# Layer 3's weight products as seven block products, new durations in the planner, and a changed merge of the left products: a four-layer graph network on one core

## The chip, the cores and the metric

The kernel runs on one core of a Trainium2 chip. Five engines work side by side: TensorE (PE, matrix products, with its own weight-load row PEld), VectorE (DVE), ScalarE (ACT), GpSimd (POOL) and SyncE (SP), whose queue here only issues DMA transfers. Each takes its instructions in a fixed order and waits on semaphores for the others. The metric is the device time of one execution, in microseconds (us); lower is better.

## The reference, cut to what matters

Sixty-four graphs of 256 nodes with 128 features (`x`, float32) pass through four layers that share one 0/1 adjacency matrix `adj` of 256 x 256. Each layer adds its result to its input and applies a layer norm. Layers 0 and 1 are attention layers, layer 2 is a gated network of five steps, layer 3 a sum of adjacency powers with weights:

```python
x = _layernorm(x + _L0_gnn_ref(x, adj, ...))      # attention over pairs
x = _layernorm(x + _L1_gnn_ref(x, adj, ...))      # attention, elu
x = _layernorm(x + _L2_gnn_ref(x, adj, adj, ...)) # five gated steps
# layer 2, one step
m_in = jnp.einsum('nm,bmd->bnd', in_matrix, h)    # adj @ h; m_out is the same
z = sigmoid(av @ w3_w.T + u3);  r = sigmoid(av @ w4_w.T + u3)
hv = tanh(av @ w5_w.T + (r * h) @ u5_w.T);  h = (1 - z) * h + z * hv
# layer 3: parts x, adj x, adj^2 x, adj^3 x, again adj x ... (adj1 is adj)
x_all = jnp.concatenate([x, chebyshev(adj, x, 3), chebyshev(adj, x, 3)], axis=3)
y = jnp.einsum('bnik,iok->bno', x_all, weight_1)  # layer norm of x + y is the output
```

With the two copies of each power put together, and the residual `x` folded into the first weight, layer 3 is y = x W0 + (A x) W1 + A^2 (x W2 + (A x) W3). The kernel forms a = A x first, then both bracketed sums with the weights, and then one product with A^2.

## The kernel before, in words

**Units and lanes.** The 64 graphs are handled in 32 units of two graphs (`UB = 2`); a unit's data is a tile of 128 partitions x 512 columns: two graphs x 256 nodes x 128 features, cut into blocks of 128 x 128. Ten lanes (`LANES`) hold the buffers of ten units in flight; unit u uses lane u mod 10. All of PSUM is eight banks of 512 columns, given to tiles by the planner.

**The planner.** The program first only lists tasks: `add(engine, ns, function, reads, writes, ...)`. `Plan.run` then lays all tasks out as a list scheduler does: for each engine it takes, among the tasks whose inputs are ready by its own clock and for which banks are free, the one with the lowest key (`first`, from the unit's number, the task's due time and `HASTE`). Its clock uses the `ns` given with each task and fixed latencies between engines. Only the order that results is written into the program: the durations in `add` are no work on the chip, but they decide where every instruction stands. `TAIL` sets how the last ten units are staggered. `PLAIN` is the number of last units that use a plain form of layer 3 (`layer3_end`).

**Seven products for eight.** A product of two matrices cut into 2 x 2 blocks takes eight block products; Winograd's form takes seven, with sums of blocks before and after. The kernel uses it for the products with A (`left_fast`, lines 838 to 861) in layer 2 and layer 3: three block sums of the data on GpSimd (`block_sums`, lines 833 to 836), seven matmuls of 128 columns (line 844), then four adds on VectorE (`merged`, lines 872 to 878), with the first product copied out of PSUM by ScalarE (line 856). The block sums of the matrix itself are made once (`fast_blocks`). The product with A^2 in layer 3 uses the same form (line 1015).

**Layer 2** (line 882 on) runs five steps per unit: A h by `left_fast`, five products of 512 columns with gate weights (line 902), three activations, four VectorE updates, and a turn of the state between node-major and feature-major by a VectorE 32 x 32 transpose and a DMA to DRAM and back. `turned` (line 537) does the same before layers 2 and 3: a transpose (line 546), one write to DRAM (line 549) and four gathers (line 552).

**Layer 3** (line 985 on), for all but the last three units: eight products of 256 columns with the two weights side by side (line 1004), into two banks; ScalarE copies the part that A^2 will multiply out of PSUM (lines 1009, 1010); VectorE makes its block sums; seven products with the blocks of A^2 (line 1015) follow, and `merged` and one more add (line 1035) put the results together. Then layer norm (`layernorm`, line 581) and the store. `layer3_end` does eight weight products (line 1048) and four of 256 columns with A^2 (line 1055).

The softmax here doesn't subtract the row's maximum and nothing guards it: scores larger than these inputs give would overflow.

## Time and profile before

| What | Value |
|---|---|
| Time, median of 3 runs | 1391.08 us (1391.00 to 1391.69) |
| The profiled execution's own time | 1392.14 us |
| Its span, first to last instruction | 1390.3 us |
| TensorE clock granted | 1.000 |
| TensorE busy | 1379.5 us (99%) |
| VectorE busy | 1217.7 us (88%) |
| ScalarE busy | 909.1 us (65%) |
| GpSimd busy | 630.5 us (45%) |
| DMA | 147 MB moved, mean 106 GB/s |

"Busy" is the time in which at least one instruction of the engine is under way. Matmuls overlap each other, so the length of a record is longer than the distance between two. A row of the groups reads: line, engine, operation, output <- inputs, shapes, count | busy us, mean ns of one | idle time of the engine just before it and what ended it. The waits list who waited for whom: us in total, times, longest. The chain that ended last follows the run back from its last instruction.

### The profile page before, as it was taken

How to read it: one execution, taken by the hardware profiler on the slowest of the kernel's cores; microseconds unless marked ns; L12 is line 12 of the kernel's file. 1: busy time of each engine (PE TensorE's matmuls, PEld its weight loads, DVE VectorE, ACT ScalarE, POOL GpSimd, SP SyncE). 2: the span in 40 equal slices, each digit the busy share in tenths (PEclk: the TensorE clock that was granted, in tenths of full speed). 3: DMA queues.
4: the chain of work that ended last, by engine and by line, in shares of the span. 5: the costliest groups of instructions: out<-in, count | busy, mean ns of one | idle time of the engine just before them, and what ended most of it. 6: DMA issues, size and time to landing. Idle time of an engine off the chain costs nothing.

```text
span 1390.3 us, 23222 instructions
## 1 busy us (share of the span) xinstructions
PE 1379.5 (99%) x6891; PEld 967.8 (70%) x6891; DVE 1217.7 (88%) x2745; ACT 909.1 (65%) x2121; POOL 630.5 (45%) x1039
## 2 busy tenths in 40 slices
PE   9999999999999999999999999999999999999998
PEld 8776666677667777667767767776666666666777
DVE  6887999999888989989898999899889798988955
ACT  6988554655676676865776768877675556564544
POOL 4233344345354453544453554465444443644524
PEclk9999999999999999999999999999999999999999
DMA  4223454445454545554554544455544545544422
GB/s 119 49 60 95 98 113 98 116 109 121 107 121 106 118 105 114 122 118 112 112 117 105 124 111 113 105 111 125 118 106 98 114 108 104 123 100 107 104 64 61
DMA packets 530076, 147.12 MB, mean 106 GB/s; under 512 B 456480, under 2 KB 495136, under 8 KB 529952
## 3 DMA queue, kind: packets, MB, share of 16 engines
q1 hardware_dynamic: 529152, 145.13, 46.5%
q8 instruction: 55, 0.90, 0.3%
q14 instruction: 69, 0.57, 0.1%
q10 hardware_dynamic: 800, 0.52, 0.1%
HBM read 81.10 MB, written 64.46 MB: 105 GB/s over the span
## 4 chain that ended last, share of the span: by engine, by line
PE 94%; DVE 3%; ACT 1%; POOL 0%; issue 0%; DMA 0%; POOLq 0%; SPq 0%; DVEq 0%; ACTq 0%
PE ps L902 48%; PE ps L844 20%; PE ps L1004 7%; PE ps L780 4%; PE ps L743 4%; PE ps L1015 3%; PE ps L792 2%; PE ps L738 2%; PE ps L667 2%; PE ps L821 1%; PE ps L1048 1%; PE ps L1055 0%; DVE st L587 0%; PE ps L351 0%; PE ps L968 0%
## 5 line engine op out<-in xcount | busy, mean ns | idle before, releaser
L902 PE MATMUL ps<-m,gT 128*128 128x512 f32 x960 | 471.5, 593 | 0.9 <-DVE m L878 0.5
L902 PEld LDWEIGHTS ps<-m,gT 128*128 128x128 f32 x960 | 170.3, 190 | 136.8 <-issue 115.9
L589 POOL TENSOR_SCALAR ve<-st 128x4 f32<-128x4 f32 x110 | 34.9, 317 | 364.9 <-DVE st L587 347.1
L914 ACT ACTIVATE e<-ps,bias 128x512 f32<-128x512 f32 x160 | 109.7, 686 | 130.2 <-PE ps L902 125.8
L931 ACT ACTIVATE p<-ps,bias 128x512 f32<-128x512 f32 x160 | 110.0, 687 | 90.3 <-PE ps L902 87.7
L592 POOL TENSOR_TENSOR rstd<-ve,nhalf 128x4 f32<-128x4 f32 x126 | 145.6, 1156 | 43.8 <-DVE ve L589 33.7
L902 PE MATMUL ps<-e,u5T 128*128 128x512 f32 x320 | 163.4, 593 | 0.0
L922 ACT ACTIVATE e<-ps,bias 128x512 f32<-128x512 f32 x160 | 109.7, 686 | 80.7 <-PE ps L902 78.6
L844 PE MATMUL ps<-adjTp,e 128*128 128x128 f32 x968 | 148.2, 275 | 0.4 <-ACT e L856 0.4
L933 DVE SCALAR_TENSOR_TENSOR p<-e,p 128x512 f32<-128x512 f32 x160 | 117.2, 733 | 33.1 <-ACT p L931 32.1
L844 PEld LDWEIGHTS ps<-adjTp,e 128*128 128x128 f32 x968 | 131.0, 192 | 19.0 <-issue 14.5
L833 POOL TENSOR_TENSOR e<-ht 128x256 f32<-128x256 f32 x121 | 99.4, 821 | 89.0 <-DMA ht<-hb 67.9
L844 PEld LDWEIGHTS ps<-adjTp,ht 128*128 128x128 f32 x726 | 108.7, 191 | 40.8 <-issue 36.7
L844 PE MATMUL ps<-adjTp,ht 128*128 128x128 f32 x726 | 120.8, 275 | 0.0
L902 PEld LDWEIGHTS ps<-e,u5T 128*128 128x128 f32 x320 | 59.2, 190 | 65.9 <-issue 50.1
L611 ACT ACTIVATE x<-ht,ve,rstd 128x128 f32<-128x128 f32 x212 | 90.9, 487 | 13.9 <-POOL ve L600 13.6
L902 PE MATMUL ps<-xT,gT 128*128 128x512 f32 x192 | 98.3, 593 | 0.5 <-DVE m L872 0.5
L833 POOL TENSOR_TENSOR e<-x 128x256 f32<-128x256 f32 x61 | 48.2, 790 | 96.2 <-ACT x L611 83.9
L875 DVE TENSOR_TENSOR m<-ps,m 128x256 f32<-128x256 f32 x182 | 74.8, 413 | 13.4 <-PE ps L844 11.1
L769 ACT ACTIVATE e<-m,esd 128x256 f32<-128x256 f32 x116 | 84.5, 765 | 0.0
L872 DVE TENSOR_TENSOR m<-ps,e 128x256 f32<-128x256 f32 x182 | 74.4, 413 | 11.2 <-PE ps L844 6.9
L835 POOL TENSOR_TENSOR e<-e,ht 128x128 f32<-128x128 f32 x121 | 79.4, 657 | 5.9
(210 smaller groups left out, 3145.7 us busy)
## 6 DMA issues: line engine op xcount, KB each, us to landing
hb<-p SPq DMA_DIRECT2D x182, 256.0 KB, 2.1
ht<-hb SPq DMA_DIRECT2D x484, 64.0 KB, 2.5
xT<-hb SPq DMA_DIRECT2D x244, 64.0 KB, 2.5
m<-row SPq DMA_DIRECT2D x58, 256.0 KB, 3.6
hb<-p SPq DMA_DIRECT2D x124, 64.0 KB, 1.8
ht<-hb SPq DMA_DIRECT2D x31, 256.0 KB, 3.0
out_dram<-x SPq DMA_DIRECT2D x30, 256.0 KB, 2.4
m<-in_x_dram SPq DMA_DIRECT2D x88, 64.0 KB, 2.3
```

The costliest lines, as they stand in the source:

```text
L592: add(POOL, 1050, lambda: nc.gpsimd.tensor_tensor(rstd.ap, ve.ap, nhalf.ap, op=ALU.pow), (ve, nhalf), (rstd,))
L611: add(ACT, 400, lambda j=j, b=b, ch=ch, view=view, at=at, shift=shift, col=col: nc.scalar.activation(X[u].ap[:, b, ch, :], view()[:, j, :] ...
L769: add(ACT, 600, lambda g=g, b=b: nc.scalar.activation(e.ap[:, g, :].rearrange("p (c n) -> p c n", c=NC), ev()[:, b], AF.Prelu, bias=esd.ap ...
L833: add(by, wide, lambda: eng.tensor_sub(four[:, 0:2], blk(slice(2, 3)).to_broadcast([P, 2, D]), blk(slice(0, 4, 3))), (src,), (s,), group=ss)
L835: add(by, narrow, lambda: eng.tensor_sub(four[:, 2:3], four[:, 1:2], blk(slice(0, 1))), (src, s), (s,), group=ss)
L844: add(PE, mm_ns(P) + 4, lambda: nc.tensor.matmul(ps.ap[:, at * P : (at + 1) * P], lhs(), mat.ap[:, k, c * P : (c + 1) * P], start=True, st ...
L902: add(PE, mm_ns(T), lambda: nc.tensor.matmul(ps.ap, w(), rhs.ap, start=start, stop=stop, skip_group_check=True), (c, rhs), (ps,), after)
L914: add(ACT, 600, lambda ps_g=ps_g, up=up: nc.scalar.activation(r.ap, ps_g.ap, AF.Tanh, bias=bias2.ap[:, 1:2], scale=0.5 / up), (ps_g, bias2 ...
L922: add(ACT, 600, lambda ps_g=ps_g, up=up: nc.scalar.activation(z.ap, ps_g.ap, AF.Tanh, bias=bias2.ap[:, 0:1], scale=0.5 / up), (ps_g, bias2 ...
L931: add(ACT, 600, lambda ps_v=ps_v, up=up: nc.scalar.activation(v.ap, ps_v.ap, AF.Tanh, bias=bias2.ap[:, 2:3], scale=1 / up), (ps_v, bias2), ...
L933: add(DVE, 600, lambda: nc.vector.scalar_tensor_tensor(v.ap, z.ap, 1.0, v.ap, op0=ALU.add, op1=ALU.mult), (v, z), (v,))
L1004: add(PE, mm_ns(N), lambda k=k, src=src, c=c, b=b, ps=ps, at=at: nc.tensor.matmul(gd(ps.ap)[:, at], bn(src.ap)[:, b, c * P : (c + 1) * P], ...
```

## The change

Five things change together.

1. Layer 3's weight products are done by seven block products too, each of 128 columns and done for the two halves of the rows (`layer3_blocks`, fourteen matmuls). The two rows of blocks are the two graphs, the inner blocks are x and A x, the two columns of blocks the two weight sums. GpSimd makes four sums of x and A x before, and VectorE four adds after them; the block sums that the A^2 product needs are now made by GpSimd. Products that are only added to each other add up in PSUM: later matmuls write without `start` onto columns that an earlier one filled, after ScalarE has copied what is needed alone. It takes four banks instead of two. The output takes five VectorE adds.
2. `left_fast` lets its second product add onto the first in PSUM, after ScalarE has copied the first out; ScalarE then copies the sum, and VectorE's first merge handles one block instead of two.
3. `turned` transposes with its input read in order and writes to DRAM by four transfers of 128-byte runs, then reads back by one plain transfer (before: one plain write, four gathers).
4. The planned durations are set anew for nearly all tasks; `TAIL` goes from 0.3 to 0.2 and `HASTE` from 10e3 to 15e3.
5. `PLAIN` goes from 3 to 4, and in `layer3_end` the two halves of a bank change places, as do the weights in `w3`.

```diff
-TAIL = 0.3
+TAIL = 0.2
...
-HASTE = {"pe": 10e3, "act": 10e3, "dve": 10e3}
-PLAIN = 3
+HASTE = {"pe": 15e3, "act": 15e3, "dve": 15e3}
+PLAIN = 4
...
+        for name, at in (("U", 0), ("p1", 2 * P)):
+            c[name] = Cell(c["z"].ap[:, at : at + 2 * P], over=[c["e"], c["z"]])
...
+    fast_blocks(w3f, w3)
...
-        add(DVE, 1050, lambda: nc.vector.transpose(
+        add(DVE, 625, lambda: nc.vector.transpose(
             v.ap.rearrange("p (a g i) -> p g a i", g=G, i=BL),
-            X[u].ap.rearrange("p b c (j a) -> p (b c) a j", j=BL)), (X[u],), (v,))
-        add("sp", 560, lambda: nc.sync.dma_start(L["hb"].ap, v.ap), (v,), (L["hb"],))
+            X[u].ap.rearrange("p b c (a j) -> p (b c) a j", j=BL)), (X[u],), (v,))
         parts = object()
         for q in range(P // BL):
-            add("sp", 640, lambda q=q: nc.sync.dma_start(
-                t.ap.rearrange("p (g q i) -> p g q i", g=G, i=BL)[:, :, q],
-                L["hb"].ap[q * BL : (q + 1) * BL].rearrange("j (a g i) -> (j a) g i", g=G, i=BL)),
-                (L["hb"],), (t,), group=parts)
+            add("sp", 560, lambda q=q: nc.sync.dma_start(
+                L["hb"].ap.rearrange("(j a) (g q i) -> q j (a g) i", a=D // BL, g=G, i=BL)[q],
+                v.ap[q * BL : (q + 1) * BL].rearrange("j (a g i) -> j (a g) i", g=G, i=BL)), (v,), (L["hb"],), group=parts)
+        add("sp", 450, lambda: nc.sync.dma_start(t.ap, L["hb"].ap.rearrange("(j a) n -> a j n", a=D // BL)), (L["hb"],), (t,))
...
-        one(x, 0, a(0), 0, 0, (src,))
-        add(ACT, 280, lambda: nc.scalar.copy(p1.ap[:, 0:P], x.ap[:, 0:P]), (x,), (p1,))
-        one(x, 1, a(1), 1, 0, (src,))
-        one(y, 3, a(3), 3, 1, (src,), s.writers[-1:])
+        one(x, 0, a(0), 0, 0, (src,), start=True)
+        held = [add(ACT, 160, lambda: nc.scalar.copy(p1.ap[:, 0:P], x.ap[:, 0:P]), (x,), (p1,))]
+        one(x, 0, a(1), 1, 0, (src,), held)
+        ms = object()
+        add(ACT, 160, lambda: nc.scalar.copy(gd(m.ap)[:, 0], x.ap[:, 0:P]), (x,), (m,), group=ms)
+        one(y, 3, a(3), 3, 1, (src,), s.writers[-1:], start=True)
...
-        merged(x, y, p1, m)
-
-    def merged(x, y, p1, m):
+        add(DVE, 200, lambda: nc.vector.tensor_add(gd(m.ap)[:, 3], gd(x.ap)[:, 2], p1.ap[:, 0:P]), (x, p1), (m,), group=ms)
+        merged(y, m, ms)
+
+    def merged(y, m, ms):
...
-        add(DVE, 400, lambda: nc.vector.tensor_tensor(
-            mv[:, 0:4:3], pv(x)[:, 1:3], p1.ap[:, 0:P].rearrange("p (o n) -> p o n", o=1).to_broadcast([P, 2, P]), op=ALU.add),
-            (x, p1), (m,))
...
-        x, y = bank(), bank()
-        home = {(0, 0): (x, slice(0, 2)), (1, 1): (x, slice(2, 4)), (0, 1): (y, slice(0, 3, 2)), (1, 0): (y, slice(1, 4, 2))}
...
+        layer3_blocks(u, L, xT, aT, tail)
+
+    def layer3_blocks(u, L, xT, aT, tail):
+        x, ya, yb, z = bank(), bank(), bank(), bank()
...
+        for k, (cell_, i, op, j, cells) in enumerate((
+                (sa, x1, ALU.subtract, x0, (xT,)), (sa, x1, ALU.subtract, a1, (xT, aT)),
+                (sb_, sums[1], ALU.subtract, x0, (sa, xT)), (sb_, sums[2], ALU.add, a0, (sb_, aT)))):
+            add(POOL, 780, lambda k=k, i=i, op=op, j=j: nc.gpsimd.tensor_tensor(sums[k], i, j, op=op), cells, (cell_,), group=group)
...
+        late = sb_.writers[-2:-1]
+        for c in range(NC):
+            one(x, 2 * c, blk(x0, c), (xT,), w3f, 0, start=not c, after=tail)
+        held = [add(ACT, 270, lambda: nc.scalar.copy(gd2(p1.ap), gd2(x.ap)[:, 0:3:2]), (x,), (p1,))]
+        for c in range(NC):
+            one(x, 2 * c, blk(a0, c), (aT,), w3f, 2, after=held)
+        for c in range(NC):
+            one(x, 2 * c + 1, blk(sums[2], c), (sb_,), w3f, 5)
+        for c in range(NC):
+            one(ya, c, blk(sums[1], c), (sa,), w3f, 4, start=not c, after=late)
...
+        for c in range(NC):
+            one(yb, NC + c, blk(a1, c), (aT,), w3f, 7)
+        m4 = gd2(mv.ap)
+        add(DVE, 335, lambda: nc.vector.tensor_add(gd2(up.ap), gd2(x.ap)[:, 1:4:2], gd2(p1.ap)), (x, p1), (up,))
+        add(DVE, 600, lambda: nc.vector.tensor_add(
+            mv.ap.rearrange("p (k n) -> p k n", k=2), ya.ap.rearrange("p (k n) -> p k n", k=2),
+            up.ap.rearrange("p (o n) -> p o n", o=1).to_broadcast([P, 2, N])), (ya, up), (mv,))
+        add(DVE, 335, lambda: nc.vector.tensor_add(up.ap, ya.ap[:, 0:N], mv.ap[:, N : 2 * N]), (ya, mv), (up,))
+        add(DVE, 600, lambda: nc.vector.tensor_add(mv.ap, yb.ap, mv.ap), (yb, mv), (mv,))
...
+        add(POOL, 780, lambda: nc.gpsimd.tensor_sub(f[:, 0:2], E[:, 4:5].to_broadcast([P, 2, P]), E[:, 0:6:5]), (mv, up), (four,), group=fs)
+        add(POOL, 580, lambda: nc.gpsimd.tensor_sub(f[:, 2:3], f[:, 1:2], E[:, 0:1]), (mv, four), (four,), group=fs)
+        add(POOL, 580, lambda: nc.gpsimd.tensor_add(f[:, 3:4], f[:, 2:3], E[:, 1:2]), (mv, four), (four,), group=fs)
...
+        one(z, 0, None, (mv,), a2f, 0, e_(0), True)
+        add(ACT, 160, lambda: nc.scalar.copy(p1.ap[:, 0:P], z.ap[:, 0:P]), (z,), (p1,))
+        done = [one(x, 0, None, (mv,), a2f, 2, e_(1)), one(x, 2, None, (four,), a2f, 3, f_(3))]
+        done = [one(x, 3, None, (up,), a2f, 7, e_(5), True, done)]
...
+        add(DVE, 335, lambda: nc.vector.tensor_add(o[:, 1:3], gd2(x.ap)[:, 2:4], o[:, 1:3]), (x, out), (out,))
+        add(DVE, 335, lambda: nc.vector.tensor_add(o[:, 2:4], o[:, 2:4], m4[:, 2:4]), (out, mv), (out,))
```

## Prediction

> **What bounds the kernel now.** I read the page first (share of each engine), then TensorE's waits, then the chain of work that ended last, then the rows of the single groups. The page's first part:
>
> ```profile
> PE 1379.5 (99%) x6891; PEld 967.8 (70%) x6891; DVE 1217.7 (88%) x2745; ACT 909.1 (65%) x2121; POOL 630.5 (45%) x1039
> ...
> PE 94%; DVE 3%; ACT 1%; POOL 0%; issue 0%; DMA 0%; POOLq 0%; SPq 0%; DVEq 0%; ACTq 0%
> PE ps L902 48%; PE ps L844 20%; PE ps L1004 7%; PE ps L780 4%; PE ps L743 4%; PE ps L1015 3%; PE ps L792 2%; PE ps L738 2%; PE ps L667 2%; PE ps L821 1%; PE ps L1048 1%; PE ps L1055 0%; DVE st L587 0%; PE ps L351 0%; PE ps L968 0%
> ```
>
> TensorE is 94% of the chain, and L1004, the line that the change replaces, 7% of it. The waits of TensorE, whole:
>
> ```profile
> PE ps L351 <- POOL ident masks.py:199: 1.3, 1, 1.3
> PE ps L792 <- DVE m L872: 0.7, 1, 0.7
> PE ps L667 <- ACT xT L535: 0.6, 1, 0.6
> PE ps L902 <- DVE m L878: 0.5, 1, 0.5
> PE ps L576 <- DVE cu L674: 0.5, 1, 0.5
> PE ps L902 <- DVE m L872: 0.5, 1, 0.5
> PE ps L844 <- ACT e L856: 0.4, 1, 0.4
> PE ps L902 <- ACT e L914: 0.2, 1, 0.2
> PE ps L792 <- ACT xT L783: 0.2, 1, 0.2
> ```
>
> Nine waits, 4.9 us (1.3 + 0.7 + 0.6 + 3 x 0.5 + 0.4 + 2 x 0.2) in 1390. About half of it lies in the first 40 us; the rest is six waits, five of them between 171 and 301 us. So almost every microsecond is a matmul being issued, and the price of a product is its spacing. The chain in order of time gives it (start, length, what):
>
> ```profile
> 143.24 3.57 PE ps L844 x32
> ...
> 278.41 3.45 PE ps L1004 x16
> ...
> 1383.19 1.15 PE ps L1055 x4
> ...
> 1384.42 0.44 DVE st L629
> ```
>
> An fp32 product is two records. A 128-column product costs 3.57/16 = 0.223 us, a 256-column product of L1004 3.45/8 = 0.431 us. The last two rows: TensorE ends at 1384.3, and about 6 us of layernorm and store follow in any case.
>
> **What the Trainium skill says.** "Trainium Kernel Development and Optimization", Performance Expectations: matmul busy time is a bad metric, because matmuls are pipelined. The trace agrees: 1379.5 us are "busy", but the products counted times their spacing (800 of 512 columns x 0.858, 450 of 256 x 0.431, 2122 of about 128 x 0.2224, 123 transposes x 0.11) are 1368, so I cost by spacing. "PSUM — Partial Sum Buffer", The four PSUM rules: a write without the first-matmul flag adds where the element was written since the last such flag, and overwrites elsewhere. So the new products can add into columns that an earlier one filled, at no extra instruction; L1015 before does the same at the plain 0.22 us. "SBUF — State Buffer", Who interferes with whom: a VectorE instruction with two SBUF inputs and a GpSimd instruction that reads SBUF exclude each other. The trace agrees: the update at L933 averages 733 ns and took 0.67 us at the quiet end of the run. "DMA: Bandwidth & Descriptors", Specifications: under 512 B a transfer is done by read-modify-write; used below as an upper bound.
>
> **The change, part by part.**
>
> *TensorE, weight products of layer 3.* Units 0 to 27 each drop eight 256-column products (3.453 us) and get fourteen of 128 columns (14 x 0.2224 = 3.114): -0.339 x 28 = -9.49 us. Unit 28 moves to the plain end form (PLAIN 3 to 4): same eight weight products, but four 256-column a2 products instead of seven blocks: 4 x 0.4315 - 7 x 0.2224 = +0.17. The seven products of `left_fast` and of a2 stay seven. Sum -9.32 us.
>
> *The second product of `left_fast` now adds onto the first one* and must let ScalarE copy the first result out. It is the only new kind of wait on TensorE in the main loop, 182 times, and all later matmuls queue behind it. The copy started 0.42 us after the issue of its product ended (1363.25 to 1363.67), lasts 0.27 (L856), and from the end of a copy to the next matmul it took 0.06 plus 0.11 of weight load (1383.13 to 1383.30): 0.86 us. Counted in the built order of the new kernel, TensorE has at least 0.88, at 5% of the places 1.08 and at the median 1.7 us of other products in between. So it fits, narrowly in some 30 places. Before, L902 behind the tanh of L914 has 31 such narrow places and one wait of 0.2 us. I take 0.3 us; from 0 to 30 x 0.15 = 4.5.
>
> *VectorE.* `left_fast`: one 256-column add (413 ns) becomes a 128-column one (279): -0.134 x 182 = -24 us. Transpose at L546: 1113 ns with strided reading; L943 reads in order and takes 701: -0.41 x 61 = -25. Layer 3: dropped 439 + 351 + 340 + 415 + 411 + 278 + 403 + 276 = 2.91 us x 29; new, by the rows of like operations, 5 x 0.413 + 2 x 0.69 + 0.28 + 0.44 = 4.17 us x 28: +32. Net -17 us before port contention.
>
> *GpSimd* gets five small operations once, for the block sums of the weights (about 2.7 us by the rows of L481 and L484, needed only at the first L1004 product, 179 us into the run), and per unit five operations of 256 columns (about 0.81) and two of 128 (0.64): 5.3 us x 28 = +149, 630 to 780 us, 56%. Its elementwise work grows from 371 to 520 us. If VectorE's loss to the shared port, 55 ns per two-input operation now, grows with it, that is +22 ns on some 830 operations: +18 us. VectorE stays where it is, near 1218 us, 88%. *ScalarE*: 182 copies more (0.27) = +48, layer 3 1.00 to 0.63 us: net +37, 68%. None of these three is on the chain; if they were, their waits would show as TensorE's.
>
> *`turned`*: one write and four gathers of 128-byte runs become four writes of 128-byte runs and one plain read. Five SP issues as before, but now one read waits for all four landings. No row shows such a write. Nearest: four writes of 512-byte runs (L961), 1.8 us; upper bound, twice the 2.5 us of the old gathers, 5 us. Path: 0.7 + 4 x 0.5 of issue + 1.8 to 5 + 3.0 (256 KB read) = 7.5 to 10.7 us; one of two writes per unit is on the way of a product. In the new order at least 11.5 us of products stand between the transpose and the first product on its result (before 12.6), 15 at a quarter of the places. Cost: zero.
>
> *PSUM*: layer 3 holds four banks instead of two, and its first one from the weight products to the end; the planner takes that into account by the order, so it costs only where the order leaves TensorE short. *New planned durations, HASTE, TAIL*: no work, another order. Reading it with the rows' durations, I find one place after the first 60 us, in the last unit, where TensorE's distance to the result it needs is shorter than the rows' sum; before there were three, two of which (285 to 288 us of TensorE work) are where waits of about 1.9 us in the list lie. I count -1.5 to +2 us, and take -0.5.
>
> *The end.* In the new order unit 27's last block product stands 16 products of 256 columns (6.9 us) before TensorE's end, against about 9.4 us for the nearest one before; its five adds, statistics, two GpSimd steps and four ScalarE scalings now stand ahead of the last unit's. Adding the rows, GpSimd is free for the last unit about 0.9 us after TensorE's end (0.8 before) and ScalarE 2.6 us after (2.1): +0.4 us.
>
> Sum: -9.3 + 0.3 - 0.5 + 0.4 = -9.1 us. The profiled execution took 1392.14 us (span 1390.3), 1.06 above the median of 1391.08; the difference is applied to the median: **1382.0 us**, and a profile near 1383.
>
> **Rivals.**
> *Waits eat part of it*: the narrow places, and GpSimd's longer queue (block sums of other units behind the four new sums, 3.2 us in a row). For: VectorE is over 90% in its dense stretches (184.65 of 200 us between 200 and 400, where TensorE waited 1.6). Against: these waits were rare at equal distance. Time: 2.5 to 6 us given back, 1384.5 to 1388.
> *Slower: VectorE sets the pace.* In the new order the densest stretch of 50 us of products (900 to 950) holds VectorE work of 57.7 us at mean row lengths; before, the densest (250 to 300) holds 55.2, and it had about 1.9 us of waits. Rows overlap (all of it sums to 1354 us, against 1217.7 busy), so this is 51.9 against 49.6 us. It decides against the change when contention adds 0.2 us to each of the 830 operations (+166 us: VectorE at 1380, as long as TensorE): then 1394 to 1402. The 22 ns worked out is a ninth of that.
> *The products do not get cheaper*: fourteen cost more than eight if one takes over 3.453/14 = 0.247 us. At 0.275, the length of a record, 3.85 x 28 would add 11 us: 1402. L844 and L1015 are the same form at 0.223, so I nearly exclude it.
> *The transposed copy comes late*: with 128-byte writes landing in over 6 us the tightest places wait; 10 places x 1 us makes 1392, no change.
>
> **How the numbers follow.** Forecast as summed (1379 to 1384.3): 0.70. Waits eat part (to 1388.3): 0.17. Within 0.2% (2.8 us, about what a measurement of this kernel tells from no change), by more of the same or by late copies: 0.06. Slower, VectorE's pace 0.05, dear products 0.01: 0.06. Below 1379: 0.01. Faster is 0.70 + 0.17 + 0.01 = 0.88. The range for 8 in 10 takes the forecast and three quarters of the next case: 1379.3 to 1387.
>
> **What would show it.** Right: the weight-product line at 0.22 us per product in the chain; TensorE's share still 99%; its waits under 8 us; the transpose near 0.7 us; GpSimd near 780 us; VectorE near 1218. Wrong: a row of TensorE waiting for the copy inside `left_fast` with tens of entries; VectorE above 1290 us; L933 above 800 ns; TensorE waiting for the transposed copy's DMA; or more than 7 us from TensorE's end to the end of the run.

## The result and the profile after

| | before | after |
|---|---|---|
| Time, median of 4 runs each on the same chip | 1391.04 us (1390.62 to 1391.69) | 1441.66 us (1441.1 to 1442.09) |
| Ratio, with its 95% interval | | 1.0363 (1.0345 to 1.0381) |
| Span of the profiled execution | 1390.3 us | 1440.2 us |
| TensorE clock granted, mean | 1.000 | 0.992 |

The changed kernel is 3.6% slower: 50.6 us above the kernel before, 59.7 us above the forecast of 1382.0.

The page of the changed kernel: busy time of the engines, then the chain that ended last, by engine and by line.

```profile
PE 1395.6 (97%) x7221; PEld 975.3 (68%) x7221; DVE 1223.9 (85%) x2765; ACT 932.0 (65%) x2274; POOL 790.5 (55%) x1240
...
PE 52%; DMA 10%; DVE 9%; ACT 5%; POOL 4%; SPq 3%; issue 2%; POOLq 0%; DVEq 0%; ACTq 0%
PE ps L909 26%; PE ps L851 11%; DMA xT<-hb 7%; PE ps L1031 6%; PE ps L750 2%; PE ps L787 2%; DVE p L940 1%; DMA m<-row 1%; PE ps L674 1%; PE ps L799 1%; PE ps L1101 1%; PE ps L745 1%; ACT e L776 1%; POOL rstd L599 1%; ACT x L618 1%
```

TensorE fell from 94% of the chain to 52%, and a transfer that stood nowhere in the list of before, `xT<-hb`, has 7%: it is the read at the end of `turned`, L562. The text on the change calls it one plain transfer, but it takes the 128 rows in the order 4 x 32. VectorE (1223.9 us) and GpSimd (790.5) are where the forecast had put them (1218 and 780), so the engines did not get more work than was counted.

The longest of TensorE's waits in the changed kernel (line waited for: us in total, times, longest):

```profile
PE ps L909 <- ACT e L921: 8.5, 5, 2.5
PE ps L851 <- ACT e L863: 6.7, 9, 1.9
PE ps L909 <- DMA xT<-hb: 6.7, 5, 2.0
PE ps L1031 <- DMA xT<-hb: 4.7, 3, 3.1
PE ps L909 <- DVE e L924: 1.9, 4, 0.9
PE ps L851 <- POOL e L843: 1.7, 2, 1.3
```

The whole list comes to 37.2 us, 4.9 before. Only 11.4 us of it name the transposed copy. The rest name ScalarE, VectorE and GpSimd. Who waits for the read itself shows why. From the answer on its line, L562, in the changed kernel (waiting instruction: us, times):

```profile
who waited for it (us, times):
  ACT p L934: 41.8, 19
  POOL p L1024: 23.0, 9
  PE ps L909: 6.7, 5
  PE ps L1031: 4.7, 3
```

ScalarE waits most, 41.8 us in 19 places. L934 is the scaled copy of the transposed data that it makes in the first gated step, for VectorE's update. GpSimd comes next with 23.0 us in 9 places: L1024 is the first sum of the new layer 3, and GpSimd's queue stands behind it. Each of them then delivers late to TensorE, and TensorE's wait is put down to ScalarE or GpSimd. So "PE waits for ACT" can be a late DMA, one step removed; how much of it is one is shown by e10 below.

The chain of the changed kernel shows the length of such a read and what is held up (start, length, what):

```profile
646.70 1.78 PE ps L1031 x16
...
761.72 8.45 DMA xT<-hb
...
770.19 0.02 ACT p L934
...
771.40 0.59 ACT e L921
...
772.03 3.27 PE ps L909 x7
```

From 761.72 to 770.17 the chain runs through one read of 256 KB: 8.45 us, its issue of 0.58 included. ScalarE's copy starts 0.02 us after it. Fourteen other reads on the chain take 5.2 to 7.6 us. The profile gives no landing times for the 61 reads of this kernel, so these are the late ones and not an average. The forecast had 3.0. The first row is the new product line: 16 records, which are 8 products of 128 columns, in 1.78 us, 0.2225 each. That is the price in the forecast.

Adding up the distances from one matmul record to the next separates the gain from the loss. At undisturbed spacing (0.429, 0.216 and 0.111 us per record of 512, 256 and 128 columns) the matmuls take 1367.7 us before and 1358.4 after, which is 9.3 us less. The distances that exceed this by over 60 ns add up to 11.5 us before (57 of them) and 69.6 after (216). The gain was made, and 58.1 us of late starts were added to it. "Late starts" below are this sum.

### The profile page after: what moved, and what is told of

The parts are those of the page before. It is cut to its first block, busy times and chain, and to the rows that moved or that the text cites. A ratio compares the mean times of both kernels' runs of the same rounds, so it can differ in the third digit from the quotient of the medians.

```text
span 1440.2 us, 24183 instructions
## 1 busy us (share of the span) xinstructions
PE 1395.6 (97%) x7221; PEld 975.3 (68%) x7221; DVE 1223.9 (85%) x2765; ACT 932.0 (65%) x2274; POOL 790.5 (55%) x1240
## 4 chain that ended last, share of the span: by engine, by line
PE 52%; DMA 10%; DVE 9%; ACT 5%; POOL 4%; SPq 3%; issue 2%; POOLq 0%; DVEq 0%; ACTq 0%
PE ps L909 26%; PE ps L851 11%; DMA xT<-hb 7%; PE ps L1031 6%; PE ps L750 2%; PE ps L787 2%; DVE p L940 1%; DMA m<-row 1%; PE ps L674 1%; PE ps L799 1%; PE ps L1101 1%; PE ps L745 1%; ACT e L776 1%; POOL rstd L599 1%; ACT x L618 1%
## 5 line engine op out<-in xcount | busy, mean ns | idle before, releaser
L909 PE MATMUL ps<-m,gT 128*128 128x512 f32 x960 | 482.9, 603 | 9.3 <-ACT e L921 8.5
L596 POOL TENSOR_SCALAR ve<-st 128x4 f32<-128x4 f32 x110 | 40.8, 372 | 256.0 <-DVE st L594 218.1
L851 PEld LDWEIGHTS ps<-adjTp,ht 128*128 128x128 f32 x726 | 120.0, 192 | 71.1 <-issue 56.5
L940 DVE SCALAR_TENSOR_TENSOR p<-e,p 128x512 f32<-128x512 f32 x160 | 124.5, 779 | 40.0 <-ACT p L938 37.1
L851 PE MATMUL ps<-adjTp,e 128*128 128x128 f32 x968 | 152.9, 277 | 2.6 <-POOL e L843 1.7
L840 POOL TENSOR_TENSOR e<-ht 128x256 f32<-128x256 f32 x121 | 103.2, 853 | 80.0 <-DMA ht<-hb 57.2
L851 PE MATMUL ps<-adjTp,ht 128*128 128x128 f32 x726 | 138.9, 277 | 5.9 <-ACT e L863 5.9
L924 DVE SCALAR_TENSOR_TENSOR e<-e,xT 128x512 f32<-128x512 f32 x96 | 68.4, 714 | 14.9 <-ACT e L921 14.9
```

The lines of the kernel that those rows point to most:

```text
L840: add(by, wide, lambda: eng.tensor_sub(four[:, 0:2], blk(slice(2, 3)).to_broadcast([P, 2, D]), blk(slice(0, 4, 3))), (src,), (s,), group=ss)
L851: add(PE, mm_ns(P) + 4, lambda: nc.tensor.matmul(ps.ap[:, at * P : (at + 1) * P], lhs(), mat.ap[:, k, c * P : (c + 1) * P], start=start, s ...
L909: add(PE, mm_ns(T), lambda: nc.tensor.matmul(ps.ap, w(), rhs.ap, start=start, stop=stop, skip_group_check=True), (c, rhs), (ps,), after)
L940: add(DVE, 640, lambda: nc.vector.scalar_tensor_tensor(v.ap, z.ap, 1.0, v.ap, op0=ALU.add, op1=ALU.mult), (v, z), (v,))
```

## The experiments

The expectations name their theories by letters. **A**: the read of L562 is slow because of its access pattern, and all else follows. **B**: the four writes of 128-byte runs land late. **C**: TensorE is held in `left_fast` by the second product that waits for ScalarE's copy. For what was left without the slow read, **D**: the new planned durations make an order that is too tight. **E**: the blocks' longer way over GpSimd, VectorE and ScalarE starves TensorE. **G**: VectorE sets the pace in dense stretches. **H**: GpSimd's longer queue does. The medians below stand beside those of the kernel before on the same chip, 1391.0 to 1391.4 us.

| run | what it is | us | ratio to before (95%) |
|---|---|---|---|
| e1_four_reads | after, the read in four | 1407.86 | 1.0122 (1.0107 to 1.0137) |
| e2_old_turn | after, `turned` of before | 1399.64 | 1.0062 (1.0047 to 1.0077) |
| e3_before_new_turn | before, new `turned` | 1426.91 | 1.0252 (1.0235 to 1.0270) |
| e5_old_left | after, `left_fast` of before | 1444.70 | 1.0379 (1.0361 to 1.0398) |
| e6_four_reads_old_left | e1 and e5 together | 1410.40 | 1.0136 (1.0119 to 1.0153) |
| e7_blocks_only | before, new layer 3 | 1410.37 | 1.0143 (1.0127 to 1.0158) |
| e8_plan_only | before, new planned durations | 1393.18 | 1.0016 (1.0009 to 1.0023) |
| e9_left_only | before, new `left_fast` | 1394.22 | 1.0025 (1.0015 to 1.0035) |
| e10_plain_read | after, the 128 rows read in their own order | 1393.53 | 1.0018 (1.0011 to 1.0026) |
| e11_plain_read_less_dve | e10, three adds left out | 1390.36 | 0.9992 (0.9983 to 1.0001) |
| e12_plain_read_less_pool | e10, GpSimd's sums an eighth as wide | 1384.71 | 0.9952 (0.9938 to 0.9967) |
| e13_old_turn_slower_plan | e2, longer planned durations | 1402.88 | 1.0082 (1.0067 to 1.0097) |
| e15_strided_plain | e10, strided transpose of before | 1400.78 | 1.0071 (1.0058 to 1.0083) |
| e16_strided_two_sums_dve | e15, two sums moved to VectorE | 1409.81 | 1.0131 (1.0115 to 1.0146) |

### Is it the transposed copy at all?

**e2_old_turn** gives the changed kernel the `turned` of before: strided transpose, one write, four gathers.

```diff
-        add(DVE, 625, ... "p b c (a j) -> p (b c) a j" ...
-        for q in range(4): add("sp", 560, ... write of 128-byte runs)
-        add("sp", 450, lambda: nc.sync.dma_start(t.ap, L["hb"].ap.rearrange("(j a) n -> a j n", a=D // BL)), ...)
+        add(DVE, 1050, ... "p b c (j a) -> p (b c) a j" ...
+        add("sp", 560, lambda: nc.sync.dma_start(L["hb"].ap, v.ap), ...)
+        for q in range(4): add("sp", 640, ... gather of 128-byte runs)
```

> The kernel after with the `turned` of before (strided transpose, one plain write, four gathers); all else of the change stays. Theories A and B: the loss goes, 1381 to 1387 us, with 25 us more VectorE time than four reads need. Theory C: 1430 us or more.

**e3_before_new_turn** is the opposite: the kernel before with the new `turned` alone, the same diff read the other way.

> The kernel before with only `turned` changed to the new one. Theories A and B: this part alone makes it slower by as much as the whole change lost against my sum, 1391 + 60 = about 1450 us, range 1430 to 1460. Theory C: 1389 to 1394 us.

Measured: e2 1399.64 us, 42.0 below the changed kernel, but 12.6 above the upper end that theories A and B expected. e3 1426.91, 35.9 above the kernel before and 3 below the range expected. The new `turned` is what costs most, with or without the rest of the change, and it is not all. In e3 the read's line, L554 there, has these waiters:

```profile
  ACT p L926: 51.2, 24
...
  PE ps L1047: 7.9, 1
...
  PE ps L901: 3.4, 4
```

It is the same picture as above, in a kernel without new products, new merging or new durations: ScalarE waits 51.2 us for the read. One wait of TensorE, 7.9 us, lies near the end, in the last units' plain form.

### Which part of it: the writes or the read?

**e1_four_reads** leaves the transpose and the writes of 128-byte runs, and splits the read into four, each of 32 whole rows, in the same place of the plan.

```diff
-        nc.sync.dma_start(t.ap, L["hb"].ap.rearrange("(j a) n -> a j n", a=D // BL))
+        rows = L["hb"].ap.rearrange("(j a) n -> a j n", a=D // BL)
+        for a in range(D // BL):
+            nc.sync.dma_start(t.ap[a * BL : (a + 1) * BL], rows[a])
```

> The kernel after, with the one read back in `turned` (128 rows of 2 KB, access pattern 4 x 32 x 512, 256 KB) issued as four reads of 32 rows each inside the same planned task; the order of everything else stays as it is in the kernel after. Theory A (the read is slow because its slowest dimension is 4, so that it runs on 4 of the 16 DMA engines, and is late for TensorE): the reads land in 2 to 4 us instead of 6 to 8, TensorE's waits fall from 36 us to under 8, the TensorE clock returns to 1.000, and the time is 1381 to 1386 us. Theory B (the four writes of 128-byte runs are what is late, or fill the DMA engines): the writes are unchanged, so at most a third of the loss comes back: 1420 to 1442 us. Theory C (the held second product of the left products makes TensorE wait): unchanged at 1436 to 1443 us.

Measured 1407.86 us, 33.8 below the changed kernel: far from theories B and C, but 21.9 above the upper end of A, and TensorE's waits still come to 16.6 us, not under 8. The answer on the read's line (L565 in e1):

```profile
  ACT p L939: 18.6, 11
  POOL p L1029: 11.0, 5
...
DMA to landing us min/median/max: 1.9/2.1/5.1
```

The same bytes arrive in 2.1 us per 64 KB, TensorE no longer waits for the copy at all, and the writes are still there. In this run the 64 KB writes (368, of which 244 are the new ones) land in 2.2 us at the median, near the lower of the two values, 1.8 and 5 us, that the prediction had put on them. But 61 x 3 further issues stand in SP's queue, of about 0.42 us each, and ScalarE and GpSimd still wait 30 us for copies. This run doesn't separate the pattern from the number of issues. The next one does.

**e10_plain_read** keeps everything: the writes, one read, and the order of all instructions on all engines. Only the pattern of the read changes, from 4 x 32 rows to 128 rows in the order in which they lie. The features then arrive in another order, so what is computed from them differs.

```diff
-        nc.sync.dma_start(t.ap, L["hb"].ap.rearrange("(j a) n -> a j n", a=D // BL))
+        nc.sync.dma_start(t.ap, L["hb"].ap)
```

> The kernel after with one access pattern changed: the read back in `turned` takes the 128 rows of the DRAM buffer in their own order (128 x 512 instead of 4 x 32 x 512), so the features of the turned tile stand in another order; same bytes, same number of issues, same order on all five engines. Theory A (4 of 16 DMA engines): the read lands in about 3 us instead of 6 to 8, TensorE never waits for it, and the time is 1392 to 1402 us (four reads gave 1407.9 with three more issues each). If the read's pattern is not the cause: 1436 to 1443.

Measured 1393.53 us: 48.1 us less than the changed kernel, from the order of one pattern's dimensions, and within A's 1392 to 1402. The read's line, L562, in e10:

```profile
  ACT p L934: 6.2, 7
  POOL p L1024: 3.9, 2
...
DMA to landing us min/median/max: 2.5/3.2/5.4
```

The read lands in 3.2 us at the median, the forecast's 3.0. ScalarE's waits for it fall from 41.8 to 6.2 us, GpSimd's from 23.0 to 3.9, TensorE's are gone. With them fall TensorE's waits that name ScalarE, from 8.5 and 6.7 us in the changed kernel to

```profile
PE ps L851 <- ACT e L863: 2.0, 3, 0.8
PE ps L909 <- ACT e L921: 0.2, 1, 0.2
```

and the whole list of its waits from 37.2 to 8.4 us. So most of what TensorE waited for ScalarE was the late read. The page of e10:

```profile
PE 1375.6 (99%) x7221; PEld 969.8 (70%) x7221; DVE 1219.2 (88%) x2765; ACT 932.7 (67%) x2274; POOL 794.6 (57%) x1240
...
PE 75%; DVE 13%; POOL 4%; DMA 3%; issue 2%; ACT 2%; SPq 1%; POOLq 0%; DVEq 0%; ACTq 0%
```

Theory A is shown as far as the pattern goes: one changed pattern gives back 48.1 us. The mechanism can be read in the Trainium skill, "DMA: Bandwidth & Descriptors", section "Why a DMA increments its semaphore by 16 and not by 1". A transfer is spread over k engines, and k is the largest number up to 16 that divides the size of the slowest dimension of both its patterns. 128 rows give 16. A pattern of 4 x 32 x 512 gives 4. The traces agree in the packets themselves. These are the reads that ran with no other packet of their size (2048 B) in the 12 us after their issue:

```
kernel   reads   2048-byte packets each   most at one time   first start to last end, us (median)
after    10      128                      5 to 6             3.1 to 5.7 (4.1)
e10       6      128                      17 to 20           1.3 to 1.7 (1.5)
```

A packet takes 0.09 to 0.12 us in both. So a single packet is no slower: a quarter to a third as many run at a time. Why the late reads take up to 8.45 us, where these quiet ones take 3.1 to 5.7, is not shown: they may stand behind other transfers on the same engines, but the trace does not say which engine a packet ran on. The slow read goes with longer waits for other transfers too: in the changed kernel SP's wait for the writes of the gated steps' transposes is

```profile
SPq L956 <- DMA hb<-p: 89.8, 42, 7.5
```

and in e10, with the same order, the same line has 69.9 us in 41 waits, the longest 4.8. Those 19.9 us are the slow read's. The larger part of the rise over the kernel before (its line L949: 37.5 us in 29 waits, the longest 3.6) is there without it.

### Was it `left_fast`?

**e5_old_left** gives the changed kernel the `left_fast` and `merged` of before (four adds, the first over 256 columns, no added product, one ScalarE copy fewer), with the new durations; **e6_four_reads_old_left** does the same to e1.

```diff
-        one(x, 0, a(1), 1, 0, (src,), held)
-        add(ACT, 160, ... gd(m.ap)[:, 0] <- x.ap[:, 0:P])
-        merged(y, m, ms)
+        one(x, 1, a(1), 1, 0, (src,))
+        merged(x, y, p1, m)        # a 256-column add first
```

> The kernel after with the left products and their merge as before (second product in its own columns, no second ScalarE copy, no product that waits for a copy); the new `turned` stays. Theories A and B: still slow, 1432 to 1446 us. Theory C: the waits of TensorE for ScalarE inside the left products vanish and the time is 1381 to 1390 us.

> The kernel after with the four reads and also the left products as before; four reads alone gave 1407.9. Theory C: it falls to 1390 to 1398. Theories D and E: within 5 us of 1407.9.

Measured 1444.70 us (3.0 above the changed kernel) and 1410.40 (2.5 above e1); single times of e5 run from 1439.78 to 1446.04, and those of e6 overlap with those of e1. Undoing the held product gains nothing in either surroundings: the lighter merging is worth at least about what its own wait costs. As the cause of the loss, C falls.

### Each part alone on the kernel before

**e7_blocks_only** adds only `layer3_blocks` (with the new durations of its own tasks, and the halves and weights of `layer3_end` that go with it), with `PLAIN` 3 and `TAIL` 0.3 as before. **e8_plan_only** changes only the planned durations, `HASTE` and `TAIL`. **e9_left_only** changes only `left_fast` and its merging, with their new durations.

```diff
# e7
-        ... eight products of 256 columns (L1004), merged, one add
+        layer3_blocks(u, L, xT, aT, tail)
# e8, durations only, for example
-TAIL = 0.3
+TAIL = 0.2
-            add(DVE, 600, ... scalar_tensor_tensor
+            add(DVE, 640, ... scalar_tensor_tensor
# e9: in substance the diff of e5, read the other way; layer 3 keeps the merging of before
```

> The kernel before with only layer 3's weight products as seven block products (with its GpSimd sums, four banks, PSUM accumulation); planned durations, TAIL, HASTE, PLAIN 3, `turned` and the left products as before. The kernel after with the old `turned` still took 1399.6 us, 18 more than the sum of the steps. Theory D (the new durations and HASTE make an order that is too tight): the blocks alone give what TensorE's work says, 1381 to 1385 us. Theory E (the blocks' longer chain over GpSimd, VectorE and ScalarE starves TensorE): 1390 to 1402 us.

> The kernel before with only the new planned durations, TAIL 0.2 and HASTE 15e3; every instruction's work is as before, only the order differs. Theory D: slower than before by 8 to 20 us, 1399 to 1411. Theory E: 1388 to 1393 us.

> The kernel before with only the left products and their merge changed (second product adds onto the first after ScalarE's copy). Theories D and E: within 3 us of before, 1388 to 1394, since VectorE's 24 us less are off the chain. Theory C, the held product: 1397 us or more.

Measured: e7 1410.37 us (+19.4), e8 1393.18 (+2.2), e9 1394.22 (+3.2). None of the parts is a gain alone. e8 is at the upper end of E's range, far from D's 8 to 20 us; e9 is 0.2 us past the range of D and E and below C's; e7 is above the ranges of both D and E. In e9 VectorE falls from 1217.7 to 1200.0 us, 17.7 where the forecast counted 24, and the time rises: here less VectorE time bought nothing, and the late starts are 14.0 us, before 11.5. In e7 the matmuls at undisturbed spacing take 1357.9 us, the gain is there, but the late starts are 37.8, and 17.5 of these lie after 1300 us. The changed kernel has 6.0 there, with the new `TAIL`, `PLAIN` and durations around the same blocks. e2, which has the `turned` of before as e7 has, differs from e7 by the new plan (durations, `HASTE`, `TAIL`, `PLAIN`) and the new `left_fast`; it has 0.9 us there and takes 10.7 us less. So around the blocks these parts together gain, though on the kernel before the durations and `left_fast` cost 2.2 and 3.2; which of them does it wasn't tried apart. The parts do not add: +35.9, +19.4, +2.2 and +3.2 are 60.7, and together they are +50.6.

### What is left over when the read is well formed

e10 is 11.5 us above the forecast. Its matmuls at undisturbed spacing take the 1358.4 us of the changed kernel, its late starts 20.3 us (98). Two runs lighten one engine each. In **e11_plain_read_less_dve** the last three adds of the blocks are not done. In **e12_plain_read_less_pool** GpSimd's four sums of layer 3 cover 32 of 256 columns.

```diff
# e11: o[:, 3:4], o[:, 1:3] and o[:, 2:4] keep their earlier values
-        add(DVE, 200, lambda: nc.vector.tensor_add(o[:, 3:4], ...
+        add(DVE, 200, lambda: None and nc.vector.tensor_add(o[:, 3:4], ...
# e12
-            ... nc.gpsimd.tensor_tensor(sums[k], i, j, op=op)
+            ... nc.gpsimd.tensor_tensor(sums[k][:, 0:32], i[:, 0:32], j[:, 0:32], op=op)
```

> As the plain read, and the last three VectorE adds of layer 3's blocks are left out (their sums are missing from the output); same order, 28 x 1.05 = 29 us less VectorE work. Theory G (VectorE sets the pace in dense stretches): at least 6 us faster than the plain read alone. Theory H (GpSimd's longer queue): within 2 us of it.

> As the plain read, and GpSimd's four new sums per unit cover 32 of their 256 columns (the rest of the sums is left as it was in the buffer); same order, about 28 x 4 x 0.55 = 62 us less GpSimd work. Theory H: at least 6 us faster than the plain read alone. Theory G: 1 to 4 us faster, since VectorE loses less to the shared port.

Measured: e11 1390.36 us (-3.2), between what G and H expected; e12 1384.71 (-8.8), as H expected. The page of e12:

```profile
PE 1371.7 (99%) x7221; PEld 968.4 (70%) x7221; DVE 1202.7 (87%) x2765; ACT 933.6 (68%) x2274; POOL 732.2 (53%) x1240
...
PE 91%; DVE 4%; DMA 1%; ACT 1%; SPq 1%; issue 1%; POOL 0%; POOLq 0%; DVEq 0%; ACTq 0%
```

With the sums cut, TensorE is again 91% of the chain, and the time is within 2.7 us of the forecast. But VectorE became shorter too, 1219.2 to 1202.7, though none of its work was taken: beside the sums on GpSimd its own instructions are longer (L940 takes 772 ns in e10, 746 in e12). So e12 takes two loads away at once.

**e13_old_turn_slower_plan** asks whether the plan is merely too tight: e2 with VectorE's updates planned at 730 instead of 640 ns and GpSimd's sums at 850 and 650 instead of 780 and 580.

```diff
-            add(DVE, 640, ... scalar_tensor_tensor    # four lines
+            add(DVE, 730, ... scalar_tensor_tensor
-            add(POOL, 780, ...                        # and 580
+            add(POOL, 850, ...                        # and 650
```

> The kernel after with the old `turned` (1399.6 us) and, in the planner alone, longer durations for what the trace shows longer than planned: VectorE's two-input updates 730 instead of 640, GpSimd's sums 850 and 650 instead of 780 and 580. If the order is too tight where VectorE and GpSimd fall behind the plan: 1384 to 1393 us. If what they lack is throughput, no order helps: 1396 to 1404.

Measured 1402.88 us, 3.2 above e2: these longer durations do not help. Other orders were not tried.

**e15_strided_plain** is e10 with the reference's outputs: the transpose reads its features in steps of four again, as before, so that the rows can be read in their own order; the planner still counts 625 ns for it, so the order is that of e10. **e16_strided_two_sums_dve** moves two narrow GpSimd sums of each last-layer group to VectorE in it, and the planner orders the tasks anew.

```diff
# e15, beside the read of e10
-            X[u].ap.rearrange("p b c (a j) -> p (b c) a j", j=BL)), (X[u],), (v,))
+            X[u].ap.rearrange("p b c (j a) -> p (b c) a j", j=BL)), (X[u],), (v,))
# e16, beside that
-        add(POOL, 580, lambda: nc.gpsimd.tensor_sub(f[:, 2:3], ...   # and tensor_add(f[:, 3:4], ...
+        add(DVE, 215, lambda: nc.vector.tensor_sub(f[:, 2:3], ...    # and tensor_add(f[:, 3:4], ...
```

> The changed kernel with the feature order of before in `turned`: VectorE's transpose reads its features in steps of four again (1113 ns in the profile of before, 695 after: 61 x 0.42 = 26 us more of VectorE), the four writes stay, and the read takes 128 rows of 512 in their own order. All outputs are the reference's. Theory A (the read's pattern) expects no wait over 4 us for the copy and a time near that of the read of whole rows alone, 1393.5 us, plus what 26 us of VectorE cost by the run that took 29 us of VectorE away (3.2 us): 1396 to 1398. A theory in which the reordering itself, and not the pattern of the read, made the gain expects about 1441.

> As e15_strided_plain, and the two narrow sums of each last-layer group that follow each other on GpSimd (L1065 and L1066, 622 and 623 ns, 28 of each: 34.9 us) are made on VectorE instead (about 0.28 us each by the row L1086 of the same width: 15.7 us). If a late GpSimd is what holds the products (the run with 62 us less of GpSimd gave 8.8 us), 35 us off its queue give 3 to 5 us: 1391 to 1394. If it is the port that both share, or VectorE as near to its own limit as GpSimd, the 15.7 us more of VectorE eat it: within 1.5 us of e15_strided_plain, or above it.

Measured: e15 1400.78 us, 7.3 above e10 and 2.8 above the upper end expected. Its read lands in 3.2 us at the median as in e10, and the theory that the reordering and not the pattern made the gain, about 1441, falls. e16 took 1409.81, 9.0 above e15, where a late GpSimd alone would have made it faster. The page of e16 and the first of TensorE's waits in it:

```profile
PE 1382.6 (98%) x7221; PEld 970.2 (69%) x7221; DVE 1260.4 (89%) x2821; ACT 933.8 (66%) x2274; POOL 757.8 (54%) x1184
```

```profile
PE ps L851 <- ACT e L863: 6.5, 8, 2.6
PE ps L909 <- DVE m L885: 5.3, 11, 1.1
```

In e15 the same two lines have 2.0 us each. GpSimd has 34.7 us less to do than in e15 and VectorE 18.5 more, and TensorE waits more for VectorE's merging (L885) and for ScalarE. Side by side, all with fourteen block products per unit and a well-formed copy:

| run | VectorE busy, us | GpSimd busy, us | late starts, us | time, us |
|---|---|---|---|---|
| e11 | 1199.1 | 792.9 | 18.1 | 1390.36 |
| e12 | 1202.7 | 732.2 | 12.3 | 1384.71 |
| e10 | 1219.2 | 794.6 | 20.3 | 1393.53 |
| e15 | 1241.9 | 792.5 | 28.2 | 1400.78 |
| e2 | 1248.7 | 788.3 | 27.9 | 1399.64 |
| e16 | 1260.4 | 757.8 | 38.6 | 1409.81 |

At the same GpSimd load (e11, e10, e15) 20.1 us of VectorE cost 3.2 us and the next 22.7 cost 7.3. The next 18.5 cost 9.0, although GpSimd got lighter (e16). That is 0.16, 0.32 and 0.49 us per us. It would fit a price that rises as VectorE fills up, but this is not shown: the three amounts stand in different places (the last adds of layer 3, the transpose ahead of the copy, the sums ahead of the A^2 products), and e16 has another order. e2, with other transfers and another order, is some 3 us below that line. e11 and e12 have nearly equal VectorE loads and differ by 5.7 us, so as an estimate the 8.8 us of e12 are about 3 of VectorE and about 6 of GpSimd's 61 us. Whether these 6 are GpSimd's queue, the shorter sums ahead of the products, or what GpSimd's sums do to VectorE's instructions is not settled, since no run changed one without the others. So 8.8 of the 11.5 us hang on the load of the helpers, spread over some 40 more small delays than before; the 2.7 left in e12 are near the 2.2 that the new durations cost alone (e8), which were not tried together.

No kernel with the reference's outputs came below the kernel before. e15 has all of the change but the transpose that reads in order, with a well-formed read, and stands at 1.0071. It is no better than e2 with the old gathers (1399.64): once the read is well formed, the reordering of `turned` brings nothing by itself. The cheaper transpose needs the features in the order in which the slow pattern, or the four reads of e1, fetch them.

## Why the prediction was wrong

**The step that failed is `turned`**, in the words of the prediction "3.0 (256 KB read)" and "Cost: zero". The 3.0 us came from the row `ht<-hb` of 256 KB in the profile of before, which reads 128 rows in order. The new read moves as many bytes by another pattern, and took 5.2 to 8.5 us on the chain. With 3.0 for it and the 2.2 us measured for the writes, the prediction's sum is 0.7 + 2.0 + 2.2 + 3.0 = 7.9 us, inside the 11.5 us of products between. With 5.2 to 8.5 it is 10.1 to 13.4, which reaches past the tightest places. The price was 48.1 us of the 59.7 missed. Two more things were missing from the sum. SP issues other transfers in between (seven at the median), so that from the end of the transpose to the issue of the read 8.0 us passed at the median, where the sum has 2.0 + 2.2; it is 8.0 in e10 too, so this is not what the 48.1 us come from, but it left less room for a slow read. And the distance was counted only to the first product, while ScalarE's copy and GpSimd's sums read the tile as well. The bound from both sides was put on the writes, which the prediction knew it had no row for, and not on the read, for which it took a row of the same bytes as a row of the same operation. The rule on k is in a page that the prediction cited, in another section.

**The rival of the late copy** named the right place with a wrong cause and a wrong size. It blamed the writes (2.2 us, not "over 6"), and priced 10 places at 1 us. TensorE waits for the copy itself in 8 places, 11.4 us; that this is near the rival's 10 is luck, since the same late copy cost 48.1. What the rival lacked is that ScalarE and GpSimd read the copy too (28 waits, 64.8 us), and the clock below.

**Weight products, -9.32**: right. 1367.7 to 1358.4 us at undisturbed spacing is -9.3, and 0.2225 us per product. The rival of dear products is out. One sum beside it was off: the products counted times their spacing, as the prediction lists them, make 1365.8 us and not 1368; nothing hangs on it.

**The held product, +0.3 (0 to 4.5)**: the waits on its two copies in `left_fast` are nine and four entries, as foreseen not tens, but 6.7 and 1.0 us in the changed kernel, above the 4.5. With the well-formed read (e10) they are 2.0 and 0.4, inside the range. Undoing it gained nothing (e5, e6). Together with the lighter merging it costs 3.2 us on the kernel before (e9), where the forecast took 0.3; about half of that are the waits on these copies (2.0 us there, 0.4 before).

**VectorE -17 and +18, GpSimd 780, ScalarE 946**: 1223.9, 790.5 and 932.0 us, so the loads were right but for 14 us of ScalarE. The groups of the transpose and the last update in the changed kernel:

```profile
L554 DVE STREAM_TRANSPOSE p<-x 128x512 f32<-128x512 f32 x61 | 42.3, 695 | 2.6 <-ACT x L618 2.4
...
L940 DVE SCALAR_TENSOR_TENSOR p<-e,p 128x512 f32<-128x512 f32 x160 | 124.5, 779 | 40.0 <-ACT p L938 37.1
```

The transpose is 0.695 us as forecast. L940 lengthened by 46 ns from 733, where 22 were worked out from GpSimd's longer time. What was wrong is the sentence that "none of these three is on the chain". That was read off the kernel before, and in e10 VectorE has 13% of the chain and GpSimd 4%. The prediction's own count had the place: 51.9 us of VectorE work for the 50 us of products from 900 on. It weighed VectorE by its sum over the whole run instead. In e10 VectorE is busy for 58.1 of the 60 us from 915 to 975, where these products lie, and late starts within them come to 2.9 us, 0.0 before. That VectorE alone makes them is not shown: e12 keeps 2.7 of them. The first rival ("waits eat part of it", 2.5 to 6 us, "GpSimd's longer queue") is in kind what e10 to e12 show, at about twice its size: 11.5 us, 8.8 of them by the helpers' load. What the four PSUM banks of layer 3 cost was not tried apart.

**Order -0.5 (-1.5 to +2)**: +2.2 alone (e8), just past the upper end and of the other sign. **The end +0.4**: from the start of TensorE's last record to the end it is 6.1 us, 6.0 before: right.

**The chances**: slower had 0.06, for VectorE's pace and dear products. The late copy stood among the cases of no change, since its price was cut off at 10 us. The signs listed under "Wrong" did name what happened: "TensorE waiting for the transposed copy's DMA".

## What to carry to other kernels

Price a DMA by its access pattern and not only by its bytes: look at the slowest dimension of both sides, because a read of 4 x 32 rows and a read of 128 rows differ here only in how the rows are counted off, and undisturbed ones took 4.1 us against 1.5 from first to last packet. When a list of TensorE's waits names ScalarE or GpSimd, ask what these waited for; one late copy was spread over rows of three engines. When counting the room for a transfer, count to every engine that reads it. And a saving on the engine that bounds the kernel is worth its sum only while the engines that pay for it have room, stretch by stretch and not on average: with VectorE at 1219 us of 1391, a further 22.7 us in the transpose cost 7.3 (e15).

## What the runs showed that was not expected

**Short starvation halved TensorE's clock.** The changed kernel has five stretches before its end in which the granted clock is 0.5, four of 3.41 us and one of 6.83; the kernel before has none. Windows of the changed kernel (span of the window: length, PE busy, PEld, DVE, ACT, POOL, clock, DMA share, GB/s):

```profile
303.00:307.00 4.00, 0.89 (x9) 0.73 (x8) 3.14 (x11) 1.77 (x6) 0.62 (x3) 1.00 0.36 68
307.00:311.00 4.00, 4.00 (x17) 2.97 (x17) 0.49 (x2) 1.40 (x4) 3.92 (x7) 0.57 0.56 87
410.00:415.00 5.00, 3.06 (x14) 1.65 (x12) 0.49 (x2) 0.80 (x3) 0.20 (x1) 1.00 0.69 205
415.00:420.00 5.00, 2.94 (x5) 1.18 (x4) 4.28 (x8) 4.41 (x10) 0.00 (x0) 0.64 0.35 65
420.00:425.00 5.00, 5.00 (x12) 2.63 (x11) 4.26 (x10) 3.90 (x6) 3.98 (x7) 0.68 0.41 95
```

After TensorE had stood still for 3.3 us from 303.4, the clock fell to a half at 307.2. After two waits of 2.0 and 2.2 us it fell for two stretches from 416.4, and twelve records took 5 us between 420 and 425, where no engine kept TensorE waiting. The Trainium skill, "TensorE: Matmul & The Clock Gate", section "Part 1: The HAM clock gate", says that an idle window of about 3.4 us halves the clock, and that the windows run freely. The length agrees (3.41 us). But TensorE need not stand still for that long: in the changed kernel a single wait of 2.0 or 2.2 us was enough three times (at 854.2, 929.3 and 1065.0 us), and e15 has such a stretch after waits of 0.5, 1.0 and 0.3 us. The late starts in the 6.9 us from the fall come to 1.3 to 1.7 us for a single stretch and 2.9 for the double one, 8.7 us in all five. So, as an estimate, about a sixth of the 48.1 us is the clock, which then runs at half speed while TensorE has work. e10 has no such stretch before its end.

**Writes of 128-byte runs were cheap.** The row of 368 writes of 64 KB in e10, of which 244 are in runs of 128 B and the others in runs of 512 B, landed in 2.2 us at the median; the 124 in runs of 512 B alone had 1.8 before. The time that the prediction had set aside for a read-modify-write, up to 5 us, is not seen.
